# Grouped-query attention in a network of eight layers: softmax factors applied to the exponentials by GpSimd before the transposes, and the products of two heads summed over all keys in the column halves

## The chip, the core and the metric

The kernel runs on one core of one Trainium2 chip. The metric is the device time of one execution in microseconds (us). Five instruction streams run side by side and wait for each other through semaphores. The profile calls them PE (TensorE, matmuls; PEld is its weight load), DVE (VectorE), ACT (ScalarE), POOL (GpSimd) and SP (SyncE, which only issues DMAs here). Each takes its own instructions in order. Matmul results are in PSUM; SBUF is the working memory.

## What is computed

The reference is a chain of eight layers (an attention-like and a feed-forward layer, four times), each followed by a residual sum and a layer norm, over 2048 tokens of width 128. All data are float32. The change touches the seventh, `_L3_attn_ref`, which attends without a mask, each query to all 2048 keys of the sequence:

```python
qkv = hidden_states @ qkv_w.T + qkv_b            # 16 query heads, 4 key and value heads of 64
xq = xq * (R_SOFTPLUS_0 / sqrt(64) * softplus(scaling))
xk = repeat(xk, 4, axis=2); xv = repeat(xv, 4, axis=2)
scores = einsum('bqhd,bkhd->bhqk', xq, xk)
probs = softmax(scores, axis=-1)
out = einsum('bhqk,bkhd->bqhd', probs, xv)
return out.reshape(B, S, 1024) @ o_w.T + o_b
```

Four query heads share one key head.

## The kernel before

The stage is the function `l3a`. It keeps everything transposed: `xT` holds the 128 features in the partitions. At first it makes the keys `kT` (64 features of a key head, twice: the keys of the first 1024 tokens in partitions 0 to 63, those of the last 1024 in 64 to 127) and the values `v` (16 tiles of 128 keys by 256).

The rest works in **units**. A unit `u` is one query head and 128 queries against all 2048 keys; a **group** `k` is the four heads `h` of one key head `g` for a tile `t` of 128 queries of a block `b` of 512. There are 256 units, 64 groups. Within a unit `c` is 0 or 1 and names a half of the keys: 512 out of each of the two halves of `kT`, so 1024.

- `scores(u, c)` multiplies queries and keys into a PSUM tile `s` of 128x1024 (L1496; two such tiles exist), and DVE takes the negated maximum over the 1024 keys (L1504, `nm`).
- `exponentials(u, c)` lets ACT compute exp(s - max of this half) into `e`, with the sum into `den` (L1510). Each half has its own maximum.
- `turn(u, c)` transposes `e` on PE into two PSUM tiles `t0` and `t1`, of which one of each exists (L1520); DVE copies one into `et` (L1522), ACT the other (L1523).
- `mixed(u)` multiplies by the values (L1535): the half c = 0 goes to the columns 0 to 63 of the array and the partitions 0 to 63 of `po`, c = 1 to the other half. The two halves of the keys stay apart, since their exponentials have different maxima. After four heads ACT copies `po` to `pos` (L1544).
- Per group five late steps bring the halves together: `factors1` to `factors3` compute for each half a factor exp(own maximum - common maximum) / common sum, on DVE, POOL and ACT with operands of 128x8 (L1552 to L1567); `divided` transposes `pos` back (four transposes, L1573), DVE multiplies by the factors (L1575), POOL adds the two halves (L1581, 128x256); `turned` transposes the result again (two transposes, L1591), and ACT copies it to `oT` (L1592).
- `out(b)` is the output projection of a block (L1598), the residual sum (L1600) and the layer norm (`finish`); `queries` makes the scaled queries of two heads (L1476, L1480), with a copy that has the partition halves exchanged by two DMAs on SP's queue.

The loop over `u` issues turn(u, 0), both scores of u + 1, the first exponential of u + 1, turn(u, 1), the second exponential, mixed(u - 1) and the late steps. No order is written by hand in this stage (others use `manual_schedule`): the scheduler of the language orders the instructions of each engine from this program order and sets the waits, and the pools set the waits for buffers.

Of the kernel before, what the change touches and what calls it, by code (L numbers as in the profile page):

```python
# [9 lines left out]
AF = mybir.ActivationFunctionType  # L10
ALU = mybir.AluOpType
AX = mybir.AxisListType
# [6 lines left out]
NB = NT // TB  # L19
# [182 lines left out]
class _Net:  # L202
# [1219 lines left out]

    def l3a(self, xT, x_new):
        nc, tc = self.nc, self.tc
        w = self.weights("w_l3a")
        wo = w[:, 1536:2560].rearrange("p (k m) -> p k m", k=8)
        rows = (slice(0, 64), slice(64, 128))
        with (  # L1430
# [6 lines left out]
            scale = self.tile(one, [128, 1], "scale")  # L1437
# [7 lines left out]
            v = self.tile(one, [128, NTILE, 256], "v")  # L1445
            for b in (0, 1):
                for g in range(4):
                    p = self.tile(ps, [128, 2, 512], "s")[:, 0, :]
                    for h, r in enumerate(rows):
# [18 lines left out]

            groups = [(b, g, t) for b in range(NB) for g in range(4) for t in range(4)]
            n = 4 * len(groups)  # L1470
            q_of, nm_of, den_of, e_of, et_of, po_of, pos_of, rec_of, on_of, oT_of = ({} for _ in range(10))

            def queries(b, c):

# [12 lines left out]
            def scores(u, c):  # L1487

                k, h = divmod(u, 4)
                b, g, t = groups[k]  # L1490
                if h == 0 and c == 0:
                    nm_of[k] = self.tile(sb, [128, 4, 2], "nm", bufs=3)
                    den_of[k] = self.tile(sb, [128, 4, 2], "den", bufs=3)
                p = self.tile(ps, [128, 2, 512], "s")
                for i, r in enumerate(rows):
                    nc.tensor.matmul(  # L1496
                        p[:, i, :],
                        lhsT=q_of[b, 4 * g + h][i][r, t * 128 : (t + 1) * 128],
                        rhs=kT[r, g, c * 512 : (c + 1) * 512],
                        start=True,  # L1500
                        stop=True,
                    )
                p = p.rearrange("p h k -> p (h k)")
                nc.vector.tensor_reduce(nm_of[k][:, h, c : c + 1], p, AX.X, ALU.max, negate=True)  # L1504
                return p

            def exponentials(u, c, p):
                k, h = divmod(u, 4)
                e = self.tile(sb, [128, 1024], f"e{c}")
                nc.scalar.activation(  # L1510
                    e, p, AF.Exp, bias=nm_of[k][:, h, c : c + 1], accum_out=den_of[k][:, h, c : c + 1]
                )
                e_of[u, c] = e

            def turn(u, c):
                e = e_of.pop((u, c))
                tp = [self.tile(pst, [128, 8, 64], f"t{i}") for i in (0, 1)]
                for j in range(8):
                    for i, r in enumerate(rows):
                        nc.tensor.transpose(tp[i][:, j, :], e[r, j * 128 : (j + 1) * 128], self.ident[r, r])  # L1520
                et = self.tile(sb, [128, 2, 8, 64], f"et{c}")
                nc.vector.tensor_copy(et[:, 0], tp[0])  # L1522
                nc.scalar.copy(et[:, 1], tp[1])  # L1523
                et_of[u, c] = et

            def mixed(u):
                k, h = divmod(u, 4)
                g = groups[k][1]
                if h == 0:
                    po_of[k] = self.tile(pso, [128, 4, 128], "po")  # L1530
                ets = [et_of.pop((u, c)) for c in (0, 1)]
                for j in range(8):
                    for c, r in enumerate(rows):
                        t = j // 4 * 8 + c * 4 + j % 4
                        nc.tensor.matmul(  # L1535
                            po_of[k][r, h, :].rearrange("p (i q) -> p i q", i=2),
                            lhsT=v[:, t, g * 64 : (g + 1) * 64],
                            rhs=ets[c][:, :, j, :],
                            start=j == 0,
                            stop=j == 7,  # L1540
                        )
                if h == 3:
                    pos_of[k] = self.tile(sb, [128, 4, 128], "pos")
                    nc.scalar.copy(pos_of[k], po_of.pop(k))  # L1544


            wide = lambda x: x.unsqueeze(2).to_broadcast([128, 4, 2])

            def factors1(k):
                nm = nm_of.pop(k)  # L1550
                m = self.tile(sb, [128, 4], "m4")
                nc.vector.tensor_reduce(m, nm, AX.X, ALU.min)  # L1552
                f = self.tile(sb, [128, 4, 2], "f8")
                nc.gpsimd.tensor_sub(f, wide(m), nm)  # L1554
                rec_of[k] = f

            def factors2(k):
                f = rec_of[k]
                nc.scalar.activation(f, f, AF.Exp)
                nc.gpsimd.tensor_mul(den_of[k], den_of[k], f)  # L1560

            def factors3(k):
                f = rec_of[k]
                m = self.tile(sb, [128, 4], "s4")
                nc.vector.tensor_reduce(m, den_of.pop(k), AX.X, ALU.add)
                nc.vector.reciprocal(m, m)
                nc.gpsimd.tensor_mul(f, f, wide(m))  # L1567

            def divided(k):
                tp = self.tile(self.ps_t, [128, 4, 128], "tp")  # L1570
                pos = pos_of.pop(k)
                for h in range(4):
                    nc.tensor.transpose(tp[:, h, :], pos[:, h, :], self.ident)  # L1573
                ot = self.tile(sb, [128, 4, 2, 64], "ot")
                nc.vector.tensor_mul(  # L1575
                    ot.rearrange("p h c d -> p (h c) d"),
                    tp.rearrange("p h (c d) -> p (h c) d", c=2),
                    rec_of.pop(k).rearrange("p h c -> p (h c)").unsqueeze(2).to_broadcast([128, 8, 64]),
                )
                on = self.tile(sb, [128, 4, 64], "on")  # L1580
                nc.gpsimd.tensor_add(on, ot[:, :, 0, :], ot[:, :, 1, :])  # L1581
                on_of[k] = on

            def turned(k):
                b, g, t = groups[k]
                if g == 0 and t == 0:
                    oT_of[b] = self.tile(one, [128, 8, 512], "oT", bufs=2)
                tp = self.tile(self.ps_t, [128, 4, 128], "tp")
                on = on_of.pop(k).rearrange("p h d -> p (h d)")
                for i in (0, 1):  # L1590
                    nc.tensor.transpose(tp[:, i, :], on[:, i * 128 : (i + 1) * 128], self.ident)  # L1591
                nc.scalar.copy(oT_of[b][:, 2 * g : 2 * g + 2, t * 128 : (t + 1) * 128], tp[:, 0:2])  # L1592
# [15 lines left out]
            for c in (0, 1):  # L1608
                exponentials(0, c, scores(0, c))
            steps = ((factors1, 3), (factors2, 4), (factors3, 5), (divided, 6), (turned, 7))  # L1610
            for u in range(n + 6):
                if u < n:
                    turn(u, 0)
                if u + 1 < n:
                    both = [scores(u + 1, c) for c in (0, 1)]
                    exponentials(u + 1, 0, both[0])
                if u < n:
                    turn(u, 1)
                if u + 1 < n:
                    exponentials(u + 1, 1, both[1])  # L1620
                if 0 < u <= n:
                    mixed(u - 1)
                for step, late in steps:
                    k, h = divmod(u - late, 4)
                    if h == 0 and 0 <= k < len(groups):
                        step(k)
                k, h = divmod(u - 9, 16)
                if h == 12 and k % 4 == 3 and k > 0:
                    out(groups[k * 4 + 3][0])
                if u % 8 == 4 and u // 8 + 2 < len(pairs):  # L1630
                    queries(*pairs[u // 8 + 2])


@with_exitstack
# [59 lines left out]
```

## Time and profile before

| | |
|---|---|
| median of 3 runs | 2825.17 us (2820.22 to 2832.1) |
| profiled execution: time, span | 2821.78 us, 2820.0 us |
| mean granted TensorE clock | 0.948 |
| first scores of the stage | 1272.1 us from the span's start |
| last output projection of the stage starts | 2649.35 us |
| POOL in 2000:2500 us | 33.17 us busy |

The span is that of one execution on the hardware profiler; its own time and the median differ by 3.4 us. A group row of the profile reads: line, engine, operation, written from read names, shapes and count, then busy time in us and mean ns of one, then the engine's idle time just before these and what ended it. For example the product by the factors that DVE makes once a group:

```profile
L1575 DVE TENSOR_TENSOR ot<-tp,f 128x512 f32<-128x512 f32 x64 | 42.4, 662 | 8.9 <-PE tp L1573 8.9
```

It ran 64 times, once a group, for 0.662 us each, and DVE stood idle 8.9 us in total before it, released by PE.

### The profile page before, as it was taken

What the parts mean: (1) busy time and instruction counts of PE and PEld (TensorE: products, weight loads), DVE (VectorE), ACT (ScalarE), POOL (GpSimd) and SP (SyncE); (2) the same over time, 40 slices, a digit from 0 to 9 for tenths busy, and PEclk for the clock granted to TensorE, in tenths of its full rate; (3) what the DMA queues carried; (4) which work ended last, traced back from release to release, by engine and by line L of the source; (5) the groups of instructions that cost most, each with busy time, mean ns of one, the idle gap of its engine ahead of it and who ended that gap; (6) DMA issues with size and microseconds to landing.
All of it is one profiled execution on the core that took longest, in us unless ns stands there. A gap on an engine that the chain in (4) does not pass through costs nothing.

```text
span 2820.0 us, 59124 instructions
## 1 busy us (share of the span) xinstructions
PE 2551.2 (90%) x24781; PEld 1613.4 (57%) x24826; DVE 1692.1 (60%) x2688; ACT 1443.1 (51%) x2520; POOL 632.9 (22%) x773
## 2 busy tenths in 40 slices
PE   5789658988977888879999999999999999999998
PEld 3466434432224555536777767777677776777543
DVE  5443243115777777647777767777677776777411
ACT  1113312225526666536766656676667665666422
POOL 2242241005667676610000000000000000000000
PEclk8569968998989999999999999999999999999999
DMA  3111100000011111010000000000000000000000
GB/s 143 40 33 37 31 21 6 0 23 8 8 47 38 33 35 53 16 51 4 9 9 6 10 7 8 9 10 6 9 6 9 9 6 9 9 6 6 1 8 8
DMA packets 30926, 55.57 MB, mean 20 GB/s; under 512 B 5387, under 2 KB 18643, under 8 KB 29379
## 3 DMA queue, kind: packets, MB, share of 16 engines
q1 hardware_dynamic: 27958, 45.09, 5.5%
q0 software_dynamic: 2272, 4.66, 0.7%
q8 instruction: 198, 3.24, 0.5%
q10 hardware_dynamic: 432, 2.04, 0.2%
q14 instruction: 66, 0.54, 0.1%
HBM read 29.49 MB, written 4.71 MB: 12 GB/s over the span
## 4 chain that ended last, share of the span: by engine, by line
PE 60%; DVE 5%; ACT 4%; POOL 2%; issue 1%; POOLq 0%; ACTq 0%; DVEq 0%
PE po L1535 17%; PE s L1496 16%; PE t L1520 11%; PE mm L849 4%; PE p L1348 2%; PE tp L1573 1%; PE tp L1476 1%; PE tp L1598 1%; PE tp L1312 1%; POOL e L1272 1%; PE tp L1591 1%; PE tp L1366 1%; DVE e L1261 1%; DVE qk L1178 1%; DVE em L1259 1%
## 5 line engine op out<-in xcount | busy, mean ns | idle before, releaser
L1510 ACT ACTIVATE e<-s,nm 128x1024 f32<-128x1024 f32 x512 | 574.2, 1121 | 394.8 <-DVE nm L1504 394.6
L1504 DVE TENSOR_REDUCE nm<-s 128x1 f32<-128x1024 f32 x512 | 602.5, 1219 | 40.3 <-PE s L1496 40.2
L1535 PE MATMUL po<-et,v 128*64 128x128 f32 x8192 | 505.7, 276 | 0.0
L1496 PE MATMUL s<-kT,qT 64*128 64x512 f32 x1024 | 495.0, 603 | 1.2 <-ACT e L1510 1.2
L1496 PE MATMUL s<-kT,qx 64*128 64x512 f32 x1024 | 494.9, 603 | 0.0
L1522 DVE COPY et<-t 128x512 f32<-128x512 f32 x512 | 350.6, 685 | 210.9 <-ACT et L1523 93.0
L1535 PEld LDWEIGHTS po<-et,v 128*64 128x64 f32 x8192 | 443.6, 137 | 17.5 <-issue 0.2
L1520 PEld LDWEIGHTS t<-con,e 64*128 64x128 f32 x8192 | 319.6, 139 | 207.4 <-issue 108.3
L1520 PE MATMUL t<-con,e 64*128 64x64 f32 x8192 | 357.7, 226 | 2.7 <-ACT e L1510 1.7
L1523 ACT COPY et<-t 128x512 f32<-128x512 f32 x512 | 301.3, 589 | 49.5 <-PE t L1520 49.5
L1554 POOL TENSOR_TENSOR f<-m,nm 128x8 f32<-128x8 f32 x64 | 12.9, 202 | 1116.1 <-DVE m L1552 1116.1
L849 PE MATMUL mm<-h,w 128*128 128x512 f32 x512 | 221.1, 592 | 0.1
L1496 PEld LDWEIGHTS s<-kT,qT 64*128 64x128 f32 x1024 | 173.4, 189 | 62.4 <-issue 52.0
L1496 PEld LDWEIGHTS s<-kT,qx 64*128 64x128 f32 x1024 | 173.3, 188 | 59.3 <-ACT e L1510 31.1
L849 PEld LDWEIGHTS mm<-h,w 128*128 128x128 f32 x512 | 97.2, 190 | 122.3 <-issue 119.4
L862 DVE SCALAR_TENSOR_TENSOR r<-mm,vec,xT 128x512 f32<-128x512 f32 x8 | 6.0, 751 | 239.8 <-PE mm L860 239.8
L856 ACT ACTIVATE h<-mm,vec 128x512 f32<-128x512 f32 x64 | 44.0, 687 | 157.3 <-PE mm L849 157.2
L284 POOL TENSOR_SCALAR ln_rs<-ln_mv 128x4 f32<-128x4 f32 x40 | 10.5, 263 | 423.4 <-DVE ln_mv L278 385.4
L1510 ACT ACTIVATION_READ_ACCUMULATOR e<-s,nm 128x1 f32 x512 | 102.8, 201 | 0.0
L299 PE MATMUL tp<-con,ln_xn 128*128 128x128 f32 x144 | 34.3, 341 | 60.5 <-issue 33.2
L1052 POOL TENSOR_TENSOR hc<-h,bc 128x1024 f32<-128x1024 f32 x32 | 75.2, 2353 | 61.2 <-PE pu L1024 31.5
L1042 DVE TENSOR_TENSOR_SCAN h<-dA,carry,pu 128x512 f32<-128x512 f32 x64 | 78.1, 1262 | 9.3 <-ACT dA L1026 8.1
(341 smaller groups left out, 3750.6 us busy)
## 6 DMA issues: line engine op xcount, KB each, us to landing
qx<-qT SPq DMA_DIRECT2D x64, 128.0 KB, 2.2
vo<-v SPq DMA_DIRECT2D x62, 128.0 KB, 2.3
ex<-in_w_ex_dram SPq DMA_DIRECT2D x4, 1536.0 KB, 15.9
rot<-in_rot_dram SPq DMA_DIRECT2D x32, 128.0 KB, 2.1
w<-in_w_l2f_dram SPq DMA_DIRECT2D x2, 1557.0 KB
w<-in_w_l1f_dram SPq DMA_DIRECT2D x1, 2816.0 KB
w<-in_w_l3f_dram SPq DMA_DIRECT2D x1, 2816.0 KB
yd<-ys SPq DMA_DIRECT2D x39, 64.0 KB, 1.5
```

Of the source, the lines that this page charges most:

```text
L849: nc.tensor.matmul(p, lhsT=hid[i][:, k, c * 128 : (c + 1) * 128], rhs=h[:, k, :], start=k == 0, stop=k == 3,)
L856: nc.scalar.activation(h_new[:, c, :], p, AF.Gelu, scale=self.v(f"{name}_{s}", c))
L1042: nc.vector.tensor_tensor_scan(h[:, i], dA[:, i], pu[i], carry_of[b - 1][:, g : g + 1], ALU.mult, ALU.add)
L1052: nc.gpsimd.tensor_mul(hc, h, bc[:, 1].unsqueeze(1).to_broadcast([128, 2, TB]))
L1348: nc.tensor.matmul(p[0:m, i * 512 : (i + 1) * 512], lhsT=w1[:, at : at + m], rhs=hn, start=True, stop=True)
L1496: nc.tensor.matmul(p[:, i, :], lhsT=q_of[b, 4 * g + h][i][r, t * 128 : (t + 1) * 128], rhs=kT[r, g, c * 512 : (c + 1) * 512], start=True, ...
L1504: nc.vector.tensor_reduce(nm_of[k][:, h, c : c + 1], p, AX.X, ALU.max, negate=True)
L1510: nc.scalar.activation(e, p, AF.Exp, bias=nm_of[k][:, h, c : c + 1], accum_out=den_of[k][:, h, c : c + 1])
L1520: nc.tensor.transpose(tp[i][:, j, :], e[r, j * 128 : (j + 1) * 128], self.ident[r, r])
L1522: nc.vector.tensor_copy(et[:, 0], tp[0])
L1523: nc.scalar.copy(et[:, 1], tp[1])
L1535: nc.tensor.matmul(po_of[k][r, h, :].rearrange("p (i q) -> p i q", i=2), lhsT=v[:, t, g * 64 : (g + 1) * 64], rhs=ets[c][:, :, j, :], star ...
```

## The change

The two halves of the keys get a common scale before the turn, so that the products of all keys can be summed in one place of PSUM.

- The second half's maximum is replaced by the common one: `scores` for c = 1 is followed by a minimum of the two negated maxima, 128x1, on DVE. The first exponential still uses its own maximum, the second uses the common one.
- After the second exponential ACT computes the factor of the first half, exp(common negated maximum - own negated maximum), 128x1.
- `divided(u)` works per unit: DVE computes the common sum, its reciprocal and the product of factor and reciprocal (three operations of 128x1), and POOL multiplies both tiles `e` of 128x1024 in place by their factors.
- `mixed(m, c)` works on two heads (a pair `m`) and one half of the keys: the two heads go to the two column halves, and all 2048 keys add up in one tile `po` of 128x128. After the second half ACT copies `po` straight to `oT`.
- `factors1` to `factors3`, the old `divided` and `turned` are gone: no transposes of the results, no DVE product and no POOL addition.
- The scores run two units ahead of the turn rather than one, with three buffers for each `e`, three for `et1` and four for the small tile `sm`, which replaces `nm` and `den`.

```diff
+                sm = sm_of[u]
...
-                nc.vector.tensor_reduce(nm_of[k][:, h, c : c + 1], p, AX.X, ALU.max, negate=True)
+                nc.vector.tensor_reduce(sm[:, c : c + 1], p, AX.X, ALU.max, negate=True)
+                if c:
+                    nc.vector.tensor_tensor(sm[:, 1:2], sm[:, 0:1], sm[:, 1:2], ALU.min)
                 return p
 
             def exponentials(u, c, p):
...
+                e = self.tile(sb, [128, 1024], f"e{c}", bufs=3)
+                nc.scalar.activation(e, p, AF.Exp, bias=sm[:, c : c + 1], accum_out=sm[:, 2 + c : 3 + c])
+                e_of[u, c] = e
+                if c:
+                    nc.scalar.activation(sm[:, 4:5], sm[:, 0:1], AF.Exp, bias=sm[:, 1:2], scale=-1.0)
+
+            def divided(u):
+                sm = sm_of.pop(u)
+                nc.vector.scalar_tensor_tensor(
+                    sm[:, 5:6], sm[:, 2:3], sm[:, 4:5], sm[:, 3:4], ALU.mult, ALU.add
                 )
-                e_of[u, c] = e
+                nc.vector.reciprocal(sm[:, 5:6], sm[:, 5:6])
+                nc.vector.tensor_mul(sm[:, 4:5], sm[:, 4:5], sm[:, 5:6])
+                for c in (0, 1):
+                    e = e_of[u, c]
+                    nc.gpsimd.tensor_mul(e, e, sm[:, 4 + c : 5 + c].to_broadcast([128, 1024]))
...
-            def mixed(u):
...
+            def mixed(m, c):
+
+                k, pair = divmod(m, 2)
+                b, g, t = groups[k]
...
+                ets = [et_of.pop((2 * m + i, c)) for i in (0, 1)]
                 for j in range(8):
-                    for c, r in enumerate(rows):
-                        t = j // 4 * 8 + c * 4 + j % 4
+                    for i, r in enumerate(rows):
                         nc.tensor.matmul(
-                            po_of[k][r, h, :].rearrange("p (i q) -> p i q", i=2),
-                            lhsT=v[:, t, g * 64 : (g + 1) * 64],
-                            rhs=ets[c][:, :, j, :],
-                            start=j == 0,
-                            stop=j == 7,
+                            po_of[m][r, :].rearrange("p (i q) -> p i q", i=2),
+                            lhsT=v[:, j // 4 * 8 + c * 4 + j % 4, g * 64 : (g + 1) * 64],
+                            rhs=ets[i][:, :, j, :],
+                            start=c == 0 and j == 0,
+                            stop=c == 1 and j == 7,
                         )
...
+                if c:
+                    nc.scalar.copy(oT_of[b][:, 2 * g + pair, t * 128 : (t + 1) * 128], po_of.pop(m))
...
+            for u in (0, 1):
+                both = [scores(u, c) for c in (0, 1)]
+                for c in (0, 1):
+                    exponentials(u, c, both[c])
+            divided(0)
+            for u in range(n + 2):
                 if u < n:
                     turn(u, 0)
-                if u + 1 < n:
-                    both = [scores(u + 1, c) for c in (0, 1)]
-                    exponentials(u + 1, 0, both[0])
+                if u + 2 < n:
+                    both = [scores(u + 2, c) for c in (0, 1)]
+                    exponentials(u + 2, 0, both[0])
                 if u < n:
                     turn(u, 1)
+                if u + 2 < n:
+                    exponentials(u + 2, 1, both[1])
                 if u + 1 < n:
-                    exponentials(u + 1, 1, both[1])
-                if 0 < u <= n:
-                    mixed(u - 1)
...
+                    divided(u + 1)
+                m, c = divmod(u - 1, 2)
+                if 0 <= m < n // 2:
+                    mixed(m, c)
```

More of the change, by code (lines that the diff above doesn't have):

```diff
@@ L1470, in l3a @@
             n = 4 * len(groups)
-            q_of, nm_of, den_of, e_of, et_of, po_of, pos_of, rec_of, on_of, oT_of = ({} for _ in range(10))
+            q_of, sm_of, e_of, et_of, po_of, oT_of = ({} for _ in range(6))
             def queries(b, c):
@@ L1490, in scores @@
                 b, g, t = groups[k]
-                if h == 0 and c == 0:
-                    nm_of[k] = self.tile(sb, [128, 4, 2], "nm", bufs=3)
-                    den_of[k] = self.tile(sb, [128, 4, 2], "den", bufs=3)
+                if c == 0:
+                    sm_of[u] = self.tile(sb, [128, 6], "sm", bufs=4)
+                sm = sm_of[u]
                 p = self.tile(ps, [128, 2, 512], "s")
@@ L1503, in scores @@
                 p = p.rearrange("p h k -> p (h k)")
-                nc.vector.tensor_reduce(nm_of[k][:, h, c : c + 1], p, AX.X, ALU.max, negate=True)
+                nc.vector.tensor_reduce(sm[:, c : c + 1], p, AX.X, ALU.max, negate=True)
+                if c:
+                    nc.vector.tensor_tensor(sm[:, 1:2], sm[:, 0:1], sm[:, 1:2], ALU.min)
                 return p
             def exponentials(u, c, p):
[L1508 to L1511, printed above, removed]
-                )
-                e_of[u, c] = e
+                sm = sm_of[u]
+                e = self.tile(sb, [128, 1024], f"e{c}", bufs=3)
[7 more added lines that the diff above has]
+                    sm[:, 5:6], sm[:, 2:3], sm[:, 4:5], sm[:, 3:4], ALU.mult, ALU.add
+                )
+                nc.vector.reciprocal(sm[:, 5:6], sm[:, 5:6])
[3 more added lines that the diff above has]
+                    nc.gpsimd.tensor_mul(e, e, sm[:, 4 + c : 5 + c].to_broadcast([128, 1024]))
             def turn(u, c):
@@ L1520, in turn @@
                         nc.tensor.transpose(tp[i][:, j, :], e[r, j * 128 : (j + 1) * 128], self.ident[r, r])
-                et = self.tile(sb, [128, 2, 8, 64], f"et{c}")
+                et = self.tile(sb, [128, 2, 8, 64], f"et{c}", bufs=2 + c)
                 nc.vector.tensor_copy(et[:, 0], tp[0])
@@ L1524, in turn @@
                 et_of[u, c] = et
-            def mixed(u):
[L1527 to L1531, printed above, removed]
+            def mixed(m, c):
+                k, pair = divmod(m, 2)
+                b, g, t = groups[k]
+                if g == 0 and t == 0 and pair == 0 and c == 0:
+                    oT_of[b] = self.tile(one, [128, 8, 512], "oT", bufs=2)
+                if c == 0:
+                    po_of[m] = self.tile(pso, [128, 128], "po")
+                ets = [et_of.pop((2 * m + i, c)) for i in (0, 1)]
@@ L1542, in mixed @@
[L1542 to L1592, printed above, removed]
+                            po_of[m][r, :].rearrange("p (i q) -> p i q", i=2),
@@ L1607, in l3a @@
                 queries(*pairs[c])
[L1608 to L1611, printed above, removed]
+            for u in (0, 1):
[4 more added lines that the diff above has]
+            for u in range(n + 2):
                 if u < n:
                     turn(u, 0)
-                if u + 1 < n:
-                    both = [scores(u + 1, c) for c in (0, 1)]
-                    exponentials(u + 1, 0, both[0])
+                if u + 2 < n:
+                    both = [scores(u + 2, c) for c in (0, 1)]
+                    exponentials(u + 2, 0, both[0])
                 if u < n:
                     turn(u, 1)
+                if u + 2 < n:
+                    exponentials(u + 2, 1, both[1])
                 if u + 1 < n:
-                    exponentials(u + 1, 1, both[1])
-                if 0 < u <= n:
-                    mixed(u - 1)
[L1623 to L1630, printed above, removed]
+                    divided(u + 1)
+                m, c = divmod(u - 1, 2)
+                if 0 <= m < n // 2:
+                    mixed(m, c)
+                k = u - 4
+                if k % 64 == 0 and k > 0:
+                    out(k // 64 - 1)
+                if u % 8 == 3 and u // 8 + 2 < len(pairs):
                     queries(*pairs[u // 8 + 2])
+            out(NB - 1)
 @with_exitstack
```

## The prediction

> **What bounds the kernel now.** I read the busy shares first, then cut the span into stretches, then the chain of waits, then the groups, and last the order of time.
>
> ```profile
> PE 2551.2 (90%) x24781; PEld 1613.4 (57%) x24826; DVE 1692.1 (60%) x2688; ACT 1443.1 (51%) x2520; POOL 632.9 (22%) x773
> ```
>
> These are averages over eight stages. The change touches one of them, so here is a stretch inside it (start:end, length, then busy time of each engine, granted clock, DMA):
>
> ```profile
> 1500.00:2000.00 500.00, 495.33 (x6768) 353.00 (x6766) 357.13 (x481) 328.21 (x628) 32.55 (x93) 1.00 0.04 8
> ```
>
> PE is busy 495 of 500 us, DVE 71%, ACT 66%, POOL 7%. The granted clock is 1.00, so no throttle enters the sum. A matmul's end is modelled, so I ask the chain of waits (start, length, what) whether PE really sets the pace:
>
> ```profile
> 2011.06 1.90 PE po L1535 x32
> 2012.95 0.64 PE t L1520 x16
> 2013.60 1.77 PE s L1496 x8
> 2015.37 0.49 PE t L1520 x16
> 2015.86 1.90 PE po L1535 x32
> ```
>
> It does: for a whole unit (one head, 128 queries) the chain never leaves PE, and the unit takes 2015.86 - 2011.06 = **4.80 us**. A group of four units also has PE work for its end, L1573 (2022.50 to 2023.08, 0.58 us) and L1591 (2007.71 to 2008.08, 0.37 us). Four units from 2000.42 to 2020.60 take 20.18 us, 5.05 each.
>
> The groups give the durations of the other engines:
>
> ```profile
> L1510 ACT ACTIVATE e<-s,nm 128x1024 f32<-128x1024 f32 x512 | 574.2, 1121 | 394.8 <-DVE nm L1504 394.6
> L1504 DVE TENSOR_REDUCE nm<-s 128x1 f32<-128x1024 f32 x512 | 602.5, 1219 | 40.3 <-PE s L1496 40.2
> ...
> L1522 DVE COPY et<-t 128x512 f32<-128x512 f32 x512 | 350.6, 685 | 210.9 <-ACT et L1523 93.0
> ```
>
> DVE has two reductions and two copies a unit: 2 x 1.219 + 2 x 0.685 = 3.81 us of 5.05. What I need from the order of time is start-to-start, which is shorter than the durations because neighbours overlap: 2.27 us for a pair of reductions (2634.67 to 2636.94), 0.60 for a copy (2636.94 to 2637.54).
>
> **What it removes, all on or beside PE's path.** Per group: four transposes (0.58 us) and two (0.37 us), the ACT copies L1544 and L1592, the DVE product L1575 (0.66), the reductions and reciprocal of the factors, and four small POOL operations. PE's part is 64 x 0.95 = 61 us. This would be the gain if PE stayed the bound. The score, turn and product matmuls keep their number and shape (16 products for each head and unit, merely paired by head).
>
> **What it adds, per unit.** DVE: a minimum (min), a scalar_tensor_tensor (STT), a reciprocal and a product, all 128x1. ACT: one more exponential of 128x1 (f), and half a copy of 128x128. POOL: two products of 128x1024. In busy time all still fits below 4.8 us: DVE 3.81 + about 0.7, ACT 4.2, POOL below 3.8. So busy time says nothing; the order does.
>
> **The order of the built program.** In the steady loop DVE runs: copy of turn(u,0); two reductions of unit u+2; copy of turn(u,1); min of u+2; STT, reciprocal, product, also of **u+2**; and then the copy of turn(u+1,0). The source writes divided(u+1) there; the built order puts the factors of u+2 right behind their own minimum (230 of the 256 units read so). Between min and STT stands ACT: the second exponential E1 needs the minimum as its bias, f follows E1, and STT needs f and the sum of E1. So DVE, which takes its instructions in order, stands still for E1 and f in every unit, and behind STT are queued the next copies, reductions and hence scores. The wait before E1 was in the old kernel too (DVE nm L1504, 394.6 us in the row above), but no DVE instruction waited for E1 then; only POOL's little factors did. The old kernel's order of time gives E1 and f:
>
> ```profile
> 2022.26 1.13 ACT L1510 ACTIVATE e<-s,nm 128x1024 f32<-128x1024 f32 x1
> ...
> 2023.27 0.21 ACT L1510 ACTIVATION_READ_ACCUMULATOR e<-s,nm 128x1 f32 x1
> 2023.36 0.21 ACT L1559 ACTIVATE f<-f 128x8 f32<-128x8 f32 x1
> 2023.65 0.20 POOL L1560 TENSOR_TENSOR den<-den,f 128x8 f32<-128x8 f32 x1 [0.98 <-ACT f L1559]
> ```
>
> The small exponential starts 1.10 us after E1 starts, takes 0.21, and its waiter starts 0.08 later.
>
> **Prices of what the trace doesn't have.** f has a bias and a scale, which L1559 has not: between 0.21 (L1559) and 0.31 (0.1 more, as L1458 with a bias takes 0.69 against 0.59 for the plain copy L1523); I take 0.29, nearer to the row with a bias. Reciprocal 128x1: L1566 (128x4) 0.178, I take 0.17. min and product: L1565 and L1552 (128x4 out) are 0.16 and 0.15, so 0.15. STT: the same plus what a scalar operand adds, 0.751 (L1600) against 0.685 for 128x512: 0.22. Between 0.10 and 0.25 for each holds all four. A dependent small operation starts 0.04 after the end of the one before (L1565 to L1566). POOL's product of a tile in place by a broadcast:
>
> ```profile
> L1183 POOL TENSOR_TENSOR qk<-qk,rq 128x1024 f32<-128x1024 f32 x32 | 75.4, 2356 | 28.2 <-DVE rq L1181 28.2
> ...
> L1272 POOL TENSOR_TENSOR e<-e,den 128x1024 f32<-128x1024 f32 x32 | 60.7, 1896 | 65.2 <-ACT rn L1207 42.4 <-DVE den L1271 17.2 <-ACT et L1281 5.5
> ```
>
> L1183 has two full inputs, L1272 is in place by a broadcast, as the new line is: 1.90. Two in a row of the like kind (L1216) take 3.77 us (853.97 to 857.74). In the built order both factors' products stand together, second half first, so the first turn waits for both; they have a whole unit for it, as they work on u+2 and are turned two units later.
>
> **Row and rule.** min, STT and the last product read two SBUF operands. What happens to such an operation while POOL computes, the first stage shows:
>
> ```profile
> 19.78 1.04 POOL L362 TENSOR_TENSOR vw<-qkv,con 128x512 f32<-128x512 f32 x1
> 19.87 0.55 DVE L346 TENSOR_TENSOR qkv<-mm,row 128x384 f32<-128x384 f32 x1
> 20.34 1.57 DVE L351 TENSOR_TENSOR qkv<-qkv,m 128x1024 f32<-128x1024 f32 x1
> ...
> 26.23 1.22 DVE L351 TENSOR_TENSOR qkv<-qkv,m 128x1024 f32<-128x1024 f32 x1
> ```
>
> L346 has one operand in PSUM and keeps its 0.55. L351 has both in SBUF: alone it takes 1.22, here 1.57, and ends 1.09 us after POOL's end at 20.82. Two more (44.65, POOL to 45.14; L356 at 50.97, POOL to 51.23) also end 1.07 and 1.08 after POOL, whatever their overlap. The Trainium skill ("SBUF — State Buffer", Who interferes with whom) says why: a VectorE instruction with two SBUF inputs and a GpSimd instruction that reads SBUF share a read interface, and the second to start is blocked until the first ends. By the busy rows alone min costs 0.15; by the rule it ends only when POOL's two products have ended.
>
> **The sum.** Without the block, DVE's ring is copy 0.60 + reductions 2.27 + copy 0.60 + min 0.15 + to ACT 0.10 (a reduction's end to E1, 2005.80 to 2005.90) + E1 1.10 + f 0.29 + 0.07 + STT 0.22 + 0.04 + reciprocal 0.17 + 0.04 + product 0.10 to the next copy = **5.75 us**. With it, POOL starts 0.10 after the product of u+1 and holds for 3.77, while DVE reaches min of u+2 after 3.5 us; min ends at 0.10 + 3.77 + 0.03, then 0.10 + 1.10 + 0.29 + 0.07 + 0.22 + 0.04 + 0.17 + 0.04 + product 0.15 = **6.08 us**. I take 6.08, as three events agree with the rule. PE has 4.8 us of work in it, ACT 4.2, POOL 3.8: all are covered. The queries (ACT 0.81, PE 0.55) fall into gaps as well, their DMAs have a lead of over eight units.
>
> Before, first scores to the start of the last output projection: 1272.1 to 2649.35, 1377.3 us. After: fill 10.5 us (scores 1.2, reductions 2.4, min to product 2.3, POOL 3.9, turn 0.7) + 254 units x 6.08 = 1544.3 + three projections inside at 11 us each = 33 (one reduction start to the next across such a one is 15.7 us at 1636.57, against 4.8) + two units without scores 6 + last product and copy 2.3 = 1596.1. Difference **+219 us**. On the profiled execution (span 2820.0, its time 2821.78, 3.4 below the median 2825.17 of the runs) that is a span of 3039 and a time of **3041 us**.
>
> **Rivals.**
> - DVE's ring without the block, 5.75 us: 254 x 0.33 = 84 less, 2957. For it: min has one element, and all three blocked events in the trace are long operations. 15%.
> - POOL pays 2.31 start-to-start for a product (L1183): ring 6.08 + 0.88 = 6.96, 254 x 0.88 = 224 more, 3265. Against it: L1216 and L1272 both have a broadcast and agree to 10 ns. 7%.
> - PE stays the bound and the change is faster: 254 x 4.80 + 51.8 of the fixed parts + 30 queries x 0.55 = 1288, 90 less, **2732**. It takes a ring below 4.8; even to break even the ring must be (1377.3 - 51.8) / 254 = 5.22. The pace is then set by POOL's 3.8 and PE together, and E1 would have to be hidden behind DVE work, which the built order excludes. 3%.
>
> The likeliest has 75%. Its own range, by the bounds of the small operations (ring 5.9 to 6.35), is 2995 to 3110. To hold 8 in 10 the low end goes to the unblocked ring: 2945 to 3110. Chances, where 0.5% (14 us) is about what a measurement can tell from no change: faster 0.03, same 0.02, slower 0.95.
>
> **What would show it.** PE's busy share in the stage falls to about 80%; the chain of waits alternates DVE and ACT (and POOL, if blocked); STT has about 1.5 us idle before it, released by ACT; min has a mean of 0.4 to 0.6 us rather than 0.15 if blocked; POOL's products stand at 1.90 us. If STT has no idle time before it, or the chain stays on PE, I am wrong.

## The result and the profile after

The change makes the kernel slower: **2976.35 us** median (2967.97 to 2988.02) against 2822.74 us of the kernel before in the same runs, a ratio of 1.0551 with a 95% interval of 1.0521 to 1.0581. The forecast was 3041 us with a range of 2945 to 3110. The profiled execution took 2976.83 us with a span of 2974.9 us (2820.0 before) and a mean granted clock of 0.948, as before.

The busy shares of the page, with instruction counts:

```profile
PE 2554.7 (86%) x24442; PEld 1553.8 (52%) x24442; DVE 1808.3 (61%) x3456; ACT 1473.2 (50%) x2712; POOL 1505.3 (51%) x1029
```

PE shows as much busy time as before (2551.2 us) in a span 155 us longer, although six transposes a group are gone; a later run takes that up. POOL has grown by 872 us. The same stretch of the stage as before, in the same columns:

```profile
1500.00:2000.00 500.00, 446.48 (x6100) 301.84 (x6096) 364.26 (x689) 312.99 (x646) 315.90 (x171) 1.00 0.03 7
```

PE fell from 495 to 446 us, 89%, and no engine is full. The clock is 1.00, so none of this is the throttle. Where no engine is full, a ring of waits sets the pace (a closed chain: each instruction waits for the one before it, and the last releases the first of the next unit), and the chain of waits names it (start, length, what):

```profile
2005.61 0.68 DVE et L1537
2006.29 2.26 DVE sm L1506 x2
2008.55 0.60 DVE et L1537
2009.15 0.29 DVE sm L1508
2009.46 0.80 ACT e L1514
2010.26 0.21 issue
2010.47 0.19 ACT e L1514
2010.66 0.19 ACT sm L1517
2010.88 0.23 DVE sm L1521
2011.13 0.17 DVE sm L1524
2011.41 0.68 DVE et L1537
```

This is one unit: 2011.41 - 2005.61 = 5.80 us, and PE is not in it. The minimum (L1508) sends the chain to ACT, for the second exponential E1 (L1514) and the small one, f (L1517), and back to the scalar_tensor_tensor STT (L1521) on DVE. The groups of the page say the same in sums:

```profile
L1528 POOL TENSOR_TENSOR e<-e,sm 128x1024 f32<-128x1024 f32 x512 | 958.5, 1893 | 575.0 <-DVE sm L1524 344.3
...
L1506 DVE TENSOR_REDUCE sm<-s 128x1 f32<-128x1024 f32 x512 | 600.5, 1214 | 2.3 <-PE s L1498 2.2
...
L1521 DVE SCALAR_TENSOR_TENSOR sm<-sm 128x1 f32<-128x1 f32 x256 | 56.1, 219 | 368.6 <-ACT sm L1517 368.6
...
L1508 DVE TENSOR_TENSOR sm<-sm 128x1 f32<-128x1 f32 x256 | 95.0, 371 | 0.1
```

DVE hardly waits for its reductions, but stands 368.6 / 256 = 1.44 us a unit before STT. POOL's products are released by L1524, the reciprocal, and not by the product of L1525 behind it; this will matter below. What the chain cannot show is why a minimum of 128x1 takes 0.29 us of it, and 0.371 us by its row. The order of time does:

```profile
2005.33 0.16 DVE L1524 RECIPROCAL sm<-sm 128x1 f32<-128x1 f32 x1
2005.53 0.16 DVE L1525 TENSOR_TENSOR sm<-sm 128x1 f32<-128x1 f32 x1
...
2005.66 3.74 POOL L1528 TENSOR_TENSOR e<-e,sm 128x1024 f32<-128x1024 f32 x2 [2.06 <-ACT et L1538]
...
2009.07 0.36 DVE L1508 TENSOR_TENSOR sm<-sm 128x1 f32<-128x1 f32 x1
2009.46 1.11 ACT L1514 ACTIVATE e<-s,sm 128x1024 f32<-128x1024 f32 x1 [0.27 <-DVE sm L1508]
```

POOL ends at 2005.66 + 3.74 = 2009.40, the minimum at 2009.07 + 0.36 = 2009.43. It is so throughout: 252 of the 256 minima begin while POOL runs a product, and each of them ends 0.01 to 0.02 us after the end of the product in which it began.

POOL's line names ACT's copy (L1538) as its releaser here. In the next unit that copy ends at 2011.485, after POOL has started at 2011.468, and in both units POOL starts 0.17 us after the end of the reciprocal; so it is the reciprocal that releases it.

From the first scores (1273.80) to the last output projection (2803.68, with two of its 16 matmuls done earlier, at 2798.35) it is 1529.9 us (1377.3 before, 1596.1 in the forecast).

### The profile page after: what moved, and what is told of

Same layout as the page of the kernel before. It is cut to its first block, busy times and chain, and to the rows that moved or that the text cites. A ratio compares the mean times of both kernels' runs of the same rounds, so it can differ in the third digit from the quotient of the medians.

```text
span 2974.9 us, 59776 instructions
## 1 busy us (share of the span) xinstructions
PE 2554.7 (86%) x24442; PEld 1553.8 (52%) x24442; DVE 1808.3 (61%) x3456; ACT 1473.2 (50%) x2712; POOL 1505.3 (51%) x1029
## 4 chain that ended last, share of the span: by engine, by line
DVE 39%; PE 15%; ACT 12%; issue 5%; POOL 2%; POOLq 0%; ACTq 0%; DVEq 0%
DVE sm L1506 19%; DVE et L1537 10%; ACT e L1514 8%; PE mm L849 4%; DVE sm L1508 2%; DVE sm L1521 2%; PE p L1348 2%; ACT sm L1517 2%; DVE sm L1524 1%; PE tp L1566 1%; PE tp L1312 1%; POOL e L1272 1%; PE po L1552 1%; PE tp L1366 1%; DVE e L1261 1%
## 5 line engine op out<-in xcount | busy, mean ns | idle before, releaser
L1528 POOL TENSOR_TENSOR e<-e,sm 128x1024 f32<-128x1024 f32 x512 | 958.5, 1893 | 575.0 <-DVE sm L1524 344.3
L1514 ACT ACTIVATE e<-s,sm 128x1024 f32<-128x1024 f32 x512 | 570.5, 1114 | 538.6 <-DVE sm L1506 464.2
L1506 DVE TENSOR_REDUCE sm<-s 128x1 f32<-128x1024 f32 x512 | 600.5, 1214 | 2.3 <-PE s L1498 2.2
L1535 PEld LDWEIGHTS t<-con,e 64*128 64x128 f32 x8192 | 298.4, 139 | 440.8 <-DVE et L1537 241.6
L1535 PE MATMUL t<-con,e 64*128 64x64 f32 x8192 | 365.5, 229 | 161.1 <-DVE sm L1508 112.6
L1538 ACT COPY et<-t 128x512 f32<-128x512 f32 x512 | 296.6, 579 | 30.7 <-PE t L1535 30.7
L1521 DVE SCALAR_TENSOR_TENSOR sm<-sm 128x1 f32<-128x1 f32 x256 | 56.1, 219 | 368.6 <-ACT sm L1517 368.6
L1514 ACT ACTIVATION_READ_ACCUMULATOR e<-s,sm 128x1 f32 x512 | 98.6, 193 | 0.0
L1508 DVE TENSOR_TENSOR sm<-sm 128x1 f32<-128x1 f32 x256 | 95.0, 371 | 0.1
```

The lines of the kernel that those rows point to most:

```text
L1506: nc.vector.tensor_reduce(sm[:, c : c + 1], p, AX.X, ALU.max, negate=True)
L1508: nc.vector.tensor_tensor(sm[:, 1:2], sm[:, 0:1], sm[:, 1:2], ALU.min)
L1514: nc.scalar.activation(e, p, AF.Exp, bias=sm[:, c : c + 1], accum_out=sm[:, 2 + c : 3 + c])
L1521: nc.vector.scalar_tensor_tensor(sm[:, 5:6], sm[:, 2:3], sm[:, 4:5], sm[:, 3:4], ALU.mult, ALU.add)
L1528: nc.gpsimd.tensor_mul(e, e, sm[:, 4 + c : 5 + c].to_broadcast([128, 1024]))
```

## The experiments

My theory after the result: the forecast's mechanism holds, which is (a) DVE's wait for E1 and f, put there by the order, and (b) the minimum held until POOL ends, with smaller terms than forecast. Rivals: (b) is no hold but a slow operation, POOL disturbs DVE or the `e` tiles in another way, or the structure itself (heads paired in the column halves, scores two units ahead) costs time. All times below are medians; ratios are against the kernel before, run on the same chip in between, with their 95% intervals.

### The minimum with one input

```diff
-                    nc.vector.tensor_tensor(sm[:, 1:2], sm[:, 0:1], sm[:, 1:2], ALU.min)
+                    nc.vector.tensor_reduce(sm[:, 1:2], sm[:, 0:2], AX.X, ALU.min)
```

The same minimum, as a reduction over two neighbouring columns: one SBUF input instead of two.

> Only the minimum of the two negated maxima is computed another way: a reduction over the two neighbouring columns (one SBUF input) in place of a tensor_tensor with two SBUF inputs; the order of all instructions stays. Theory (the minimum is held until GpSimd's two products end, and this is in DVE's ring): the minimum falls from 0.36 to about 0.15 us, the unit from 5.80 to 5.60 to 5.65 us, the time by 38 to 53 us to 2923 to 2938. Rival (0.36 us is what this operation costs, or its length is not in the ring): the time stays at 2976 within 10 us.

Measured: **2923.24 us**, ratio 1.0356 [1.0310, 1.0403], the unit 5.59 us. Its order of time, with POOL's products and then the minimum:

```profile
2099.71 3.75 POOL L1528 TENSOR_TENSOR e<-e,sm 128x1024 f32<-128x1024 f32 x2 [1.84 <-DVE sm L1524]
...
2103.11 0.14 DVE L1508 TENSOR_REDUCE sm<-sm 128x1 f32<-128x2 f32 x1
```

POOL runs until 2103.46, and the minimum begins and ends inside of that in 0.14 us. So the hold is real, the form with one SBUF input does not have it, and it costs 5.80 - 5.59 = 0.21 us a unit; 254 x 0.21 = 53 us is the whole difference of the times. The run changes the kind of operation together with the number of inputs; the last section has events that separate the two.

### POOL's products left out

```diff
                 nc.vector.tensor_mul(sm[:, 4:5], sm[:, 4:5], sm[:, 5:6])
-                for c in (0, 1):
-                    e = e_of[u, c]
-                    nc.gpsimd.tensor_mul(e, e, sm[:, 4 + c : 5 + c].to_broadcast([128, 1024]))
```

> GpSimd's two products are left out, so the exponentials are summed without their factors; all small operations and their waits stay. Theory (GpSimd costs only by holding the minimum): the same unit as with a one-input minimum, 5.6 us, time 2915 to 2930. Rival (GpSimd's 3.74 us is itself in the ring, between the factors and the turn): the unit falls well below 5.5 us, time below 2890. Rival (GpSimd is covered altogether): 2976.

Measured: **2914.75 us**, ratio 1.0323 [1.0282, 1.0364], the unit 5.60 us. The two-input minimum is now short (0.148 us in the stretch from 1700 to 2500 us):

```profile
L1508 DVE TENSOR_TENSOR sm<-sm 128x1 f32<-128x1 f32 x139 | 20.6, 148 | 0.0
```

The wait before STT, over the whole run, stands unchanged:

```profile
L1521 DVE SCALAR_TENSOR_TENSOR sm<-sm 128x1 f32<-128x1 f32 x256 | 56.1, 219 | 369.0 <-ACT sm L1517 368.9
```

The reductions keep their 1.214 us with and without POOL. So the new POOL work cost 62 us here, against 53 us for the hold alone in the run before; the two intervals overlap, so that no other cost of it is shown. What is left of the loss stands with the wait for E1.

### Everything new but the structure left out

```diff
-                if c:
-                    nc.vector.tensor_tensor(sm[:, 1:2], sm[:, 0:1], sm[:, 1:2], ALU.min)
...
-                if c:
-                    nc.scalar.activation(sm[:, 4:5], sm[:, 0:1], AF.Exp, bias=sm[:, 1:2], scale=-1.0)
...
                 sm = sm_of.pop(u)
-                nc.vector.scalar_tensor_tensor(
...
-                    nc.gpsimd.tensor_mul(e, e, sm[:, 4 + c : 5 + c].to_broadcast([128, 1024]))
```

The minimum, f and the whole rest of `divided` are out; each half keeps its own maximum.

> The new arrangement of the products without any factors: the minimum, the factor's exponential, the three small operations and GpSimd's products are left out, so that each half keeps its own maximum and nothing is divided. Theory (what the removed transposes free on TensorE is real, and only what was added covers it): TensorE sets the pace at 4.8 us a unit, time 2735 to 2760. Rival (the pairing of the heads itself costs, by a single output tile in PSUM or later copies): above 2800.

Measured: **2750.36 us**, ratio 0.9749 [0.9734, 0.9764]. Its chain of waits:

```profile
2101.64 1.90 PE po L1540 x32
2103.53 0.64 PE t L1523 x16
2104.18 1.77 PE s L1498 x8
2105.95 0.49 PE t L1523 x16
2106.44 1.90 PE po L1540 x32
```

PE is the bound again at 4.80 us a unit, and the six transposes of each group are gone: the structure gains 72 us. PE's busy time is 2489.5 us here for the same 24442 matmuls that show 2554.7 in the changed kernel, so its sum there hid the work that is gone. The sum does not follow the time that PE waits: the run with the longest waits below (3178 us) shows 2502.3 us, with 45 matmul records missing. Why it differs stays open. With these runs the loss can be added up: -72 (structure) + 164 (2750 to 2915: the small operations and the wait for E1) + 62 (2915 to 2976: the hold) = +154 us. The parts are differences along one chain of runs, so they add up to the measured loss by construction; the middle one does not part the small operations from the wait.

### The order that the source writes

```diff
+            with tc.manual_schedule(engines=MAIN):
...
                     turn(u, 0)
+                    divided(u + 1)
...
                     exponentials(u + 2, 1, both[1])
-                if u + 1 < n:
-                    divided(u + 1)
```

With a fixed order, STT to product of the next unit stand behind the first turn, so that E1 and f have most of a unit.

> The order is written by hand: the three small operations that make the factors of unit u+1 stand behind the first copy of turn(u, 0), a whole iteration after their exponentials, instead of directly behind their own minimum; the products stand first half first. Nothing else changes. Theory: DVE no longer waits for the second exponential (its idle time before the scalar_tensor_tensor goes from 369 us to near 0), but GpSimd now starts later against the minimum, about 1.3 us after the first copy starts, and holds the minimum until about 5.1 us, so that the unit is still 5.6 to 5.75 us: time 2935 to 2965. Rival (the wait for the exponential alone made the loss, nothing holds the minimum): PE sets the pace at 4.8 us a unit, time 2730 to 2750.

A miss: **3178.27 us**, ratio 1.1275 [1.1231, 1.1318], 202 us slower than the changed kernel. The order of time of this kernel:

```profile
2100.04 3.75 POOL L1528 TENSOR_TENSOR e<-e,sm 128x1024 f32<-128x1024 f32 x2 [2.83 <-DVE sm L1525]
2102.20 1.60 DVE L1508 TENSOR_TENSOR sm<-sm 128x1 f32<-128x1 f32 x1
2103.72 0.68 DVE L1537 COPY et<-t 128x512 f32<-128x512 f32 x1
2105.26 0.69 DVE L1537 COPY et<-t 128x512 f32<-128x512 f32 x1 [0.86 <-PE t L1535]
```

The wait for E1 is gone and the hold has grown to 1.60 us, both as expected: DVE reaches the minimum sooner, POOL's end does not move with it. Overlooked was the third wait. There is one PSUM buffer of each transposed tile, so the turn's next half can start only when the copy is out, and the copy of that half only 0.14 + 0.73 us later. DVE now stands idle for these 0.86 us. In the changed kernel they lay behind the minimum and the wait for E1. The unit is 6.58 us.

The same order with all three operations on one SBUF tensor input:

```diff
+                    nc.vector.tensor_reduce(sm[:, 1:2], sm[:, 0:2], AX.X, ALU.min)
...
+                nc.vector.tensor_scalar(sm[:, 5:6], sm[:, 2:3], sm[:, 4:5], sm[:, 3:4], ALU.mult, ALU.add)
                 nc.vector.reciprocal(sm[:, 5:6], sm[:, 5:6])
+                nc.vector.tensor_scalar(sm[:, 4:5], sm[:, 4:5], sm[:, 5:6], None, ALU.mult)
```

> The hand-written order of the previous kernel, and the three small operations with two SBUF inputs each written with one (the minimum as a reduction, the sum and the product as tensor_scalar with operands of 128x1 per partition). Theory: neither the wait for the exponential nor GpSimd's hold is left in DVE's ring (4.2 us), PE sets the pace at 4.8 us a unit: time 2730 to 2760, 2 to 3.5% below the kernel before. Rival (the two-input form does not matter): the same time as the kernel with the order alone.

Measured: **2859.67 us**, ratio 1.0139 [1.0102, 1.0177], another miss, between the two times expected. It is 319 us below the run before, with a minimum of 0.15 us instead of 1.60: the hold was most of what that run lost. The unit is 5.23 us and not 4.8, and the chain shows the same 0.86 us (L1533 the transposes, L1535 the copies):

```profile
2103.77 2.35 DVE sm L1506 x2
2106.15 0.15 DVE sm L1508
2106.30 0.61 DVE et L1535
2106.91 0.14 issue
2107.05 0.73 PE t L1533 x16
2107.78 0.68 DVE et L1535
```

### Scores three units ahead

```diff
-                    if u + 1 < n:
-                        divided(u + 1)
-                    if u + 2 < n:
-                        both = [scores(u + 2, c) for c in (0, 1)]
+                    if u + 3 < n:
+                        both = [scores(u + 3, c) for c in (0, 1)]
...
+                    if u + 2 < n:
+                        divided(u + 2)
```

The code is set against the hand-written order above. `divided(u + 2)` stands behind the copy of turn(u, 1) and thus in the gap, one unit later than E1 of its unit. `sm` has five buffers.

> Order by hand with scores three units ahead of the turn: the small operations that make the factors of unit u+2 stand between the second copy of turn(u, 1) and the first of turn(u+1, 0), where DVE has to wait 0.86 us for the transposes anyway, and their exponentials are one iteration old; all three take one SBUF input. Theory (three things were in DVE's ring: the wait for the exponential, GpSimd's hold, and the transposes between the two copies): DVE's ring is 0.68 + 2.35 + 0.15 + 0.61 + 0.87 = 4.66 us, below TensorE's 4.8, so the time is 2740 to 2775. Rival (something else, such as ScalarE or the single PSUM buffers of the transposes, holds the unit near 5.2 us): about 2850.

> The same order as the previous kernel, the three small operations in their original form with two SBUF inputs. Theory: GpSimd's products start just as the first copy starts and hold the minimum until 3.7 us, 0.65 us after DVE reaches it; the minimum has a mean near 0.7 us, the unit is about 5.2 us, time 2800 to 2850. Rival (the hold is covered, since DVE has room): the same time as the previous kernel.

Measured: **2809.70 us**, ratio 0.9955 [0.9941, 0.9969], with one input, a miss; **2818.39 us**, ratio 0.9983 [0.9968, 0.9997], with the two inputs of the changed kernel, inside what was expected but not for the reason given. The second has the very instructions of the changed kernel and is 158 us faster: that much was order and lead, the hold included. Its minimum has a median of 0.159 us and so almost no hold, against my theory's 0.7: POOL starts at 2100.35 for 3.75 us and the minimum ends at 2104.12, 0.02 after POOL, since in this order DVE gets there just as POOL ends. The rest of the miss of the one-input run is a ring that I had not seen:

```profile
2104.12 0.61 DVE et L1535
2104.73 0.14 issue
2104.86 0.71 PE t L1533 x16
2105.57 0.93 PE s L1498 x4
...
2106.60 2.37 DVE sm L1506 x2
2108.96 0.02 issue
2108.99 0.15 DVE sm L1508
2109.14 0.61 DVE et L1535
```

The copy frees the PSUM tile of the next first turn, behind which PE has the scores, which the reductions need, behind which stands the next copy: 5.02 us, with PE and DVE in turn.

### Four more orders

Each one was to break the ring of the one before, with one-input operations unless said. Each of the one-input runs was expected between 2745 and 2790 us, and each missed.

The copy of the second turn between the two reductions:

```diff
                         both = [scores(u + 3, c) for c in (0, 1)]
+                        maximum(u + 3, 0, both[0])
                         exponentials(u + 3, 0, both[0])
                     if u < n:
                         turn(u, 1)
                     if u + 3 < n:
+                        maximum(u + 3, 1, both[1])
                         exponentials(u + 3, 1, both[1])
```

`maximum` is the reduction and the minimum, taken out of `scores`. The second run of these two has the two-input operations again.

> As the kernel three units ahead with one-input operations, but DVE takes the copy of turn(u, 1) between the two reductions instead of behind both and the minimum. Theory (what held the unit at 5.02 us was the ring turn 0.71, first scores 0.93, two reductions 2.37, minimum 0.17, copy 0.61, 0.14 back to the turn, through the single PSUM buffer of the transposes): the copy no longer waits for the second reduction, the ring falls below TensorE's 4.8 us, the time is 2750 to 2775. Rival (GpSimd's or ScalarE's order holds the unit): it stays near 2810.

> The same with the original two-input operations. Theory: GpSimd's products now end before DVE reaches the next minimum, so nothing is held (a minimum of 0.15 to 0.2 us) and the time equals the one-input kernel's within 10 us. Rival (the hold comes back): 20 us or more above it.

Measured: **2810.62 us**, ratio 0.9947 [0.9928, 0.9966], and **2821.18 us**, 0.9989 [0.9973, 1.0004], with two inputs. In the second only 2 of the 256 minima begin inside a product, so the hold is gone as expected; the difference of 10.6 us, at the edge of the 10 expected, is not explained by it. The chain is all PE at 5.02 us, but the scores take 1.99 us instead of 1.77: their second half waits 0.11 us for the PSUM tile that E1 of the unit before frees, and the first matmuls after the wait stand 0.53 us apart instead of 0.43.

The first half of the scores ahead of the first turn, the second behind it, so that the second half no longer waits for E1:

```diff
+                    if u + 3 < n:
+                        p0 = scores(u + 3, 0)
                     if u < n:
                         turn(u, 0)
...
+                        p1 = scores(u + 3, 1)
```

> One-input operations, scores three units ahead, and the first half's scores of unit u+3 now stand ahead of turn(u, 0) on TensorE; DVE takes both reductions and the minimum before the copy of turn(u, 1), as in the kernel three units ahead. Theory (two rings held 5.02 us in the last two orders: turn, first scores, reductions, copy, turn in one; second exponential, second scores, turn, copy, second reduction, minimum in the other; with the scores ahead of the turn the first ring loses its scores and reductions, and the second exponential has the whole first half of the next unit before its scores are overwritten): TensorE sets the pace at 4.8 to 4.9 us a unit, time 2750 to 2785. Rival (GpSimd's products or ScalarE's 4.2 us of work hold the unit at 5.0 us): 2810.

Measured: **2819.91 us**, ratio 1.0000 [0.9983, 1.0018]. No step in its chain is a wait, and the unit is still 5.03 us:

```profile
2102.15 1.06 PE s L1498 x4
2103.21 0.50 PE t L1535 x16
2103.71 0.91 PE s L1498 x4
2104.62 0.66 PE t L1535 x16
2105.28 1.90 PE po L1552 x32
2107.18 1.06 PE s L1498 x4
```

The same eight matmuls take 1.06 + 0.91 = 1.97 us here, with transposes between the two halves, and 1.77 together in the run without factors; that is most of the 0.23 us by which the unit is above 4.80.

Scores together, the products by the values between the two turns, again with a lead of two units. Buffers and the places where `queries` is called change with it:

```diff
+                    if u + 2 < n:
+                        both = [scores(u + 2, c) for c in (0, 1)]
+                    if u + 1 < n:
+                        divided(u + 1)
+                    if u + 2 < n:
+                        maximum(u + 2, 0, both[0])
+                        exponentials(u + 2, 0, both[0])
+                        maximum(u + 2, 1, both[1])
                     if u < n:
                         turn(u, 0)
...
+                    m, c = divmod(u - 2, 2)
                     if 0 <= m < n // 2:
                         mixed(m, c)
+                    if u < n:
+                        turn(u, 1)
```

> One-input operations, scores two units ahead, and another round trip on TensorE: both scores of unit u+2 together, turn(u, 0), the products of the unit before (they lag one unit more, with three buffers for each et and three instead of four for the queries), then turn(u, 1). Each copy out of the transposes' single PSUM buffers now has other TensorE work beside it, and the two scores stay adjacent, which the last two orders had split at 0.2 us a unit (1.97 to 1.99 us against 1.77). Theory (TensorE's 4.8 us is then the only bound; GpSimd's 3.7 us is covered): time 2745 to 2780, 1.5 to 2.7% below the kernel before. Rival (any order with GpSimd's products ends at 5.0 us a unit, so they do cost beyond what the rings explain): 2805 to 2825.

And with one thing moved:

```diff
-                    if u + 1 < n:
-                        divided(u + 1)
...
                         turn(u, 0)
+                    if u + 1 < n:
+                        divided(u + 1)
```

> The order of e11 with one thing moved: the reciprocal and product of the factors of the next unit (divided) stand directly behind the first half's turn, so VectorE has them between its two copies, in the 0.86 us in which TensorE makes the second half's transposes. Theory (e11's ring was the second copy, the two reductions, the minimum, the first copy, and then the transposes with nothing beside them and the small operations after the second copy): the ring is copy .68 + .1 + reductions 2.35 + minimum .17 + copy .61 + transposes .86 = 4.8 us a unit, as much as TensorE has to do; time 2750 to 2790. Rival (GpSimd's products now begin later and their first one ends just as the next unit's turn is due, or TensorE's own pass costs 5.0 us in whatever order its parts stand): 5.0 us a unit or more, time 2805 to 2830.

Measured: **2871.76 us**, ratio 1.0174 [1.0150, 1.0198], and **2835.07 us**, ratio 1.0044 [1.0030, 1.0059]. In the first the small operations stood behind both copies, so DVE waited out the transposes: the unit is 5.23 us again. In the second they fill that gap, but release POOL later, and the rival came true, with a unit of 5.08 us in the median and a time just above the rival's. Its chain runs over two units:

```profile
2107.14 0.22 DVE sm L1525
...
2107.50 1.90 POOL e L1528
2109.39 0.04 issue
2109.44 0.71 PE t L1535 x16
```

The next turn waits for POOL's first product. Between L1525 here and the one before (2102.01) are 5.13 us.

## Why the forecast was right, and where 64 us went

**Right: the built order is the cause.** In the trace the minimum, STT, the reciprocal and the product follow each other on DVE in 250 of the 256 units, as was read before. The chain alternates DVE and ACT, and STT waits 1.44 us (forecast 1.5). Changing only order and lead brings back 158 us, all of the loss of 154; the hold's part is in it, since the minimum then meets POOL's end. Taking the wait for E1 away by order alone did not help: that run lost 202 us more, to a longer hold and the wait for transposes. PE is left with gaps as said, but at 89% busy rather than 80%: the shorter ring alone makes it 4.80 / 5.80 = 83%, and I had counted neither the queries and projections nor that PE's busy sum would be 65 us higher than without the new work. The bound of the optimistic rival, 2732, was near (2750 without the new work), but no run reached it with all the work.

**Right: rule over row for the minimum.** The busy rows gave 0.15 us, the Trainium skill ("SBUF — State Buffer", Who interferes with whom) an end with POOL's. The trace has the end 0.01 to 0.02 us after POOL's (0.03 from the rounded row), a mean of 0.371 us (forecast 0.4 to 0.6), and up to 1.591; the one-input form is not held. The case against it, that the operation has one element in a partition, did not count. Two points of the forecast did not come. POOL was to be in the chain of waits if it blocked, but the held time stands in the minimum's own record, and the unit's chain has no POOL. And the hold was to last until both products end, but it lasts until the end of the one under way: a minimum that began in a first product (at 1281.61 in the changed kernel) ended at 1282.29 with it (1282.27), while the second ran on. In all other held minima it was the second anyway.

**Mis-sized: the ring, 6.08 us against 5.80.** The step most in error is "POOL starts 0.10 after the product of u+1". I had written that the second half's product stands first on POOL, but not drawn from it that this one needs the reciprocal alone. It starts 0.17 us after the reciprocal, before L1525 has ended; the sum had 0.04 + 0.15 + 0.10 = 0.29 there. The terms of the blocked ring, measured from the rows shown above and the next unit:

| term | forecast | measured |
|---|---|---|
| minimum's end to E1 | 0.10 | 0.03 |
| E1's start to f, f | 1.10 + 0.29 | 1.10 + 0.28 |
| to STT, STT | 0.07 + 0.22 | 0.04 + 0.22 |
| to the reciprocal, reciprocal | 0.04 + 0.17 | 0.03 + 0.16 |
| to POOL's start | 0.29 | 0.17 |
| POOL's two products | 3.77 | 3.74 |
| POOL's end to the minimum's end | 0.03 | 0.03 |
| sum | 6.08 | 5.80 |

254 x 0.28 = 71 us; the fixed parts came out some 5 us above their sum, and the span 64 us below the forecast's 3039. The ring without the hold is 5.60 (products left out) against 5.75: the minimum starts beside the end of the copy and adds 0.08 us instead of 0.15, and it releases E1 in 0.02 us instead of 0.10, both by that run's chain of waits. Both rings were too long by the same kind of error: gaps between dependent small operations, taken from one reduction to its exponential.

**In range with some luck.** The forecast's own range for the blocked ring was 5.9 to 6.35 us, 2995 to 3110 us of time, and the measured 5.80 and 2976 lie below it. The stated range held the time only because its low end, 2945, had been set for the unblocked rival.

**What the time alone would have said.** The rival without the hold gave 2957, and 2976 lies nearer to it than to 3041. By the time alone the wrong mechanism looks right; the first two experiments and the end of the minimum decide.

**Open.** No run with the whole work came to 4.80 us a unit. Each order after the first met another ring, or in one case longer matmuls, between 5.02 and 5.23, and whether an order or more PSUM for the transposed tiles avoids all of them was not tried. The two best versions, both with one-input operations and scores three units ahead (2809.70 and 2810.62 us), beat both kernels, the one before by some 0.5%, which is at the edge of what a measurement can tell.

## What to carry to other kernels

A change that takes 61 us from the bounding engine and puts its new work on idle ones can still lose 154: draw the ring of waits in the order that the program is built with, for each in-order engine, before adding up busy time. A small operation that depends on another engine belongs as far behind its producer as buffers allow, and taking one wait away exposes the one that it covered (here 0.86 us of transposes), so name that one first. Where a small VectorE operation would begin while GpSimd works long on SBUF, give it one SBUF input: for the minimum that alone was worth 53 us here.

## What the hardware showed beyond that

- The hold does not show as idle time: the minimum's own record grows, to 1.60 us for one element in a partition when DVE comes early. In the changed kernel 252 minima began inside a GpSimd product, in the first hand-written order 255, and each ended 0.01 to 0.02 us after that product.
- The number of SBUF inputs decides, as far as the events go. The product of L1525 (two SBUF inputs, otherwise 0.16 us) once began inside a GpSimd product of the changed kernel: it took 1.02 us and ended at 1293.76, GpSimd at 1293.74. With one SBUF tensor input, a `tensor_scalar` at 2640.41 and one at 2640.91 in the one-input run three units ahead lay inside a GpSimd product (2639.84 to 2641.73) and took 0.27 and 0.21 us, as elsewhere.
- ACT started E1 0.03 us after the end of the minimum in the changed kernel, held, and in the first two runs, not held; but 0.09 us after it in the first hand-written order, and 0.10 us after a reduction in the kernel before. What makes the difference is open.
- VectorE's reductions from PSUM took 1.214 us with GpSimd busy and without it.
- On TensorE, the two halves of the scores cost 0.2 us more with transposes between them (1.97 against 1.77 us, in the one run with that order).
- TensorE's busy time for the same matmuls was 2489.5 us in one order of waits and 2554.7 in another; it is no measure of the work alone.
